# One scan for both values of a step, and an accumulating DMA for the token stream

## The chip, the cores and the metric

The kernel runs on one core of a Trainium2 chip. Times are device microseconds (us). The time before is 2727.75 us, the median of 3 runs (2727.06 to 2733.11).

## What is computed

Two layers work on x of 8 batches x 512 tokens x 256 features, all in float32. Each adds an attention part and a feed-forward part to its input. The change is in the attention part of the first layer, a linear recurrence that runs over the tokens in both directions:

```python
dx = conv(x) - x                                  # neighbours, per feature
t5 = tanh((x + dx * maa_x) @ maa_w1)              # five groups of 32
xw, xk, xv, xr, xg = (x + dx * (maa_f + t5[f] @ maa_w2[f]) for f in range(5))
r, k, v, g = xr @ Wr, xk @ Wk, xv @ Wv, silu(xg @ Wg)
d = exp(-exp(time_decay + tanh(xw @ decay_w1) @ decay_w2))
# forward, per head: S = d_t * S + k_t v_t ; y_f = r_t S
# backward:          y_b = r_t S ; S = d_t * (S + k_t v_t)
y = y_f + y_b
out = (group_norm(y * sigmoid(dx @ gate_w + gate_b)) * g) @ Wo
```

There are 16 heads of 16 x 16 state. Beside it the first layer has 8 experts, of which each token uses 2. The second layer has two softmax attentions and 16 small experts.

## The kernel before

Five queues run in their written order: PE (TensorE), DVE (VectorE), ACT (ScalarE) and SP (SyncE, which issues DMAs) are pinned to the order in which the code records instructions; POOL (GpSimd) is not, and a scheduler places its instructions. Work is written as Python generators. `Turns.turn` moves each running generator to its next `yield`, so a turn decides what stands beside what in each queue, and the number of `yield`s between a producer and a consumer says how much other work is put between them.

The first layer's spine is `scans`. Features lie on partitions, tokens run along the free dimension. A step treats one batch b, one half c of the 256 features and one pair vg of the 16 value columns of a head: 8 x 2 x 8 = 128 steps. In a step, SP's eight DMAs of `spread` (L878) have brought the two values of each head to its 16 partitions as `kv`, 128 x 2 x 512. DVE multiplies by k (L901), then for each of the two values runs a forward scan with the factors `dq` (L910) and a backward scan with the decays `d` (L914), and multiplies by r (L923). The two scans together give the sum of both directions up to factors that k and `dq` hold. PE then adds up over the 16 partitions of each head (`sums`, L929). A step has four `yield`s, so four turns.

Beside the scans run: `experts`, 39 chunks of 256 routed tokens, with weights that POOL gathers from memory by indirect DMA (`wgu`, `wdn` L567, tokens `xs` L577), products on PE (L615, L655), silu on ACT (L639), products on DVE (L624); `projections(b + 1)`, which prepares the next batch one part after the other (`inputs`, `values`, `decays`); and `ending`, which normalises a finished half and multiplies it by g on POOL (L987).

`projections` is what the change touches. `mixed` makes the inputs xw ... xg: PE's product goes to PSUM (L732, L734), DVE computes (product + maa) * dx into a tile `xf` of 128 x 512 (L739), and POOL adds the token stream xT to it (L742). Two turns later PE reads the tiles: `dw` (L815) reads xw, and `project` (L697) makes r, v, k and g of the others. `values` calls `mixed` for xv and xk, `decays` for xw and xr, and later for xg. `decays` makes `d` on ACT (L829, L830), with one column more that holds 0 for the last token, and `dq` on DVE (L848 to L854). Batch 0 is prepared before the scans begin; there the mixing tiles lie in buffers of the pool `held`, and the routing and its `turn_round` (a table of which token is in which slot, made by comparing and multiplying one-hot tiles `ls` and `hs`) go through DVE, ACT and PE too. `entry` starts the second layer: it gathers each token's two expert rows as `y0`.

Of the kernel before, what the change touches and what calls it, by code (L numbers as in the profile page):

```python
# [26 lines left out]
F32 = mybir.dt.float32  # L27
# [9 lines left out]
P = 128  # L37
B, T, D = 8, 512, 256
NC = D // P
# [126 lines left out]
def two_layers(ctx: ExitStack, tc: tile.TileContext, a: dict, out: bass.AP):  # L166
# [106 lines left out]
    def entry(b):  # L273
# [7 lines left out]
        for t0 in range(0, NT, ahead):  # L281
            ys = []
            for t in range(t0, t0 + ahead):
                y = temp([P, 2, D], "y0", f"y0_{b}_{t}", ahead)
                n = b * NT + t
                for i in range(2):
                    pool_e.indirect_dma_start(
                        out=y[:, i, :], out_offset=None, in_=outs,
                        in_offset=bass.IndirectOffsetOnAxis(ap=slot[i][:, n : n + 1], axis=0),
                    )  # L290
                ys.append((t, n, y))
            yield
# [79 lines left out]
    with ExitStack() as l0:  # L372
# [142 lines left out]
        def turn_round():  # L515
# [18 lines left out]
            for k in range(NTT // 4 + 1):  # L534
# [9 lines left out]
                if k < NTT // 4:  # L544
                    ls = held(k % 4, [P, 2, 4, P], f"ls{k}")
                    hs = held(4 + k % 4, [P, 2, 4, n2], f"hs{k}")
                    for i in range(2):
                        for o, of in ((ls, low), (hs, high)):
                            n = o.shape[3]
                            vec_e.tensor_tensor(  # L550
                                o[:, i], bc(of[i][:, 4 * k : 4 * k + 4], 2, n),
                                bc(C["count"][:, :n], 1, 4), ALU.is_equal,
                            )
                    for j in range(4):
                        n = 4 * k + j
# [114 lines left out]
        made = {}  # L670

        def projections(b):

# [13 lines left out]

            def mix(name, i, other=False):
                if other and first:
                    return held(i, [P, T], f"{name}_{b}")  # L690
                return rw.tile([P, T], F32, tag="xf", name=f"{name}_{b}", bufs=4)

# [29 lines left out]
            def mixed(*fs, other=False):  # L722

                xs = {f: [] for f in fs}
                for c in range(NC):
# [10 lines left out]
                    yield  # L736
                    for f, ps in zip(fs, pss):
                        t = mix(f"xf{f}{c}", 2 * c + (f != fs[0]), other)
                        vec_e.scalar_tensor_tensor(  # L739
                            t, ps, V("maa_" + "wkvrg"[f], c), dxs[c], ALU.add, ALU.mult  # L740
                        )
                        pool_e.tensor_tensor(t, t, xT[c], ALU.add)  # L742
                        xs[f].append(t)
                yield
                yield
                return [xs[f] for f in fs]

            def inputs():
# [13 lines left out]
                for _ in range(0 if first else 1):  # L762
                    yield
                xxx = []
                for c in range(NC):
                    t = mix(f"xxx{c}", c)
                    vec_e.scalar_tensor_tensor(t, dxs[c], V("maa_x", c), xT[c], ALU.mult, ALU.add)
                    xxx.append(t)
                for _ in range(1 if first else 2):
# [37 lines left out]
            def decays():  # L807
                yield from until("inputs", b)
                d = rw.tile([P, NC, T + 1], F32, tag="d", name=f"d_{b}", bufs=2)
                vec_e.memset(d[:, :, T:], 0.0)  # L810
# [17 lines left out]
                for co in range(NC):  # L828
                    act_e.activation(dT[:, co, :], pss[co], AF.Exp, bias=V("time_decay", co))  # L829
                act_e.activation(dT, dT, AF.Exp, scale=-1.0)  # L830
                for _ in range(1 if first else 2):
                    yield
# [5 lines left out]

                near = [mix(f"near{c}", 4 + c, True) for c in range(NC)]
                for c in range(NC):  # L840
# [3 lines left out]
                for _ in range(1 if first else 2):  # L844
                    yield
                dq = big("dq")
                for c in range(NC):
# [5 lines left out]
                vec_e.scalar_tensor_tensor(dq, dq, -1.0, q[:, :, 1:], ALU.mult, ALU.mult)  # L853
                vec_e.tensor_tensor(dq, dq, dT, ALU.mult)  # L854
                yield
                yield from until("keys", b)
                k = made[b]["k"]
                vec_e.tensor_tensor(k, k, q[:, :, 1:], ALU.mult)
                made[b].update(d=d, dq=dq, r=r)
                done.add(("scans", b))  # L860
# [8 lines left out]

        NV = 2  # L870
        STEPS = P // (P // HD) // NV

        def spread(b, c, vg):

            kv = rw.tile([P, NV, T], F32, tag="kv", name=f"kv{c}{vg}_{b}", bufs=4)
            for hh in range(P // HD):
                row = c * P + hh * HD + vg * NV
                nc.sync.dma_start(  # L878
                    kv[hh * HD : (hh + 1) * HD], bc(made[b]["vd"][row : row + NV, :], 0, HD)
                )  # L880
            return kv


# [3 lines left out]
        def scans(turns):  # L887
# [4 lines left out]
            for n, (b, c, vg) in enumerate(todo):  # L892
                if c == vg == 0:
                    x = rw.tile([P, NT, D], F32, tag="x", name=f"x_{b}")
                    z = rw.tile([P, NC, T], F32, tag="z", name=f"z_{b}")
                    if b + 1 < B:
                        turns.add(then(*projections(b + 1)))
                k, d, dq, r = (made[b][n] for n in ("k", "d", "dq", "r"))
                dc, qc, kc, rc = d[:, c, 1:], dq[:, c, :], k[:, c, :], r[:, c, :]
                kv = kvs.pop((b, c, vg))  # L900
# [7 lines left out]
                yield  # L908
                for i in range(NV):
                    vec_e.tensor_tensor_scan(  # L910
                        out=kv[:, i, :], data0=qc, data1=kv[:, i, :], initial=0.0,
                        op0=ALU.mult, op1=ALU.add,
                    )
                    vec_e.tensor_tensor_scan(  # L914
                        out=kv[:, i, ::-1], data0=dc[:, ::-1], data1=kv[:, i, ::-1],
                        initial=0.0, op0=ALU.mult, op1=ALU.add,
                    )
                    if i == 0 and len(late) == 2:
                        for sums in late:
                            sums()  # L920
                        late = []
                    yield
                vec_e.tensor_tensor(kv, kv, bc(rc, 1, NV), ALU.mult)  # L923
# [96 lines left out]
        def begin():  # L1020
# [8 lines left out]
            tag_of = {  # L1029
                "y0": ("xf", 4), "gt4": ("t5a", 1), "eq4": ("th", 1), "gt16": ("dx", 1),  # L1030
                "eq16": ("xnT", 1), "cT": ("xf", 4),
            }
# [511 lines left out]
```

## Time and profile before

| what | value |
|---|---|
| median of 3 runs | 2727.75 us |
| the profiled execution | 2728.59 us |
| its span, first to last instruction | 2726.8 us |
| PE, DVE, ACT, POOL busy | 2362.4, 2157.0, 888.3, 477.5 us |
| scans L914 and L910 | 336.7 and 320.0 us on DVE, 256 instructions each |
| multiplications L901 and L923 | 172.0 and 162.9 us on DVE, 128 each |
| additions L742 | 113.3 us on POOL, 80 |
| mean granted PE clock | 0.916 |

A line of the profile names the source line, the engine, the operation and the tiles (written <- read). Where it has a bar, the busy time and the mean duration of one follow, then the idle time of the engine before it and what ended it. A wait line names who waited for whom, the total in us, the number of times and the longest. The rows of digits cut the span into 40 equal slices of 68 us, and each digit is the busy share in tenths.

### The profile page before, as it was taken

Reading aid. Unit: us, or ns where it says so; the run is one execution under the profiler, and the core shown is the slowest. Engines: PE = TensorE matmul, PEld = TensorE weight load, DVE = VectorE, ACT = ScalarE, POOL = GpSimd, SP = SyncE. Lnnn points to the kernel's source line nnn. Section 1 sums busy time; section 2 is a strip of 40 time slices with the busy share of each in tenths; the row PEclk is TensorE's granted clock in tenths of the full one; section 3 lists DMA queues with packets and bytes.
Section 4 is the critical chain, followed back from the end, with each engine's and each line's share of the span. In section 5 each row is a group of like instructions: output and inputs, shape, how many; then the busy total and the mean of one; then the engine's idle time right before and its main releaser. Section 6 shows DMA issues by size and latency. Waiting matters only on the chain.

```text
span 2726.8 us, 32763 instructions
## 1 busy us (share of the span) xinstructions
PE 2362.4 (87%) x11900; PEld 1412.8 (52%) x11900; DVE 2157.0 (79%) x3063; ACT 888.3 (33%) x1687; POOL 477.5 (18%) x441
## 2 busy tenths in 40 slices
PE   6699898988989889898826899999989989898996
PEld 4355555555556545555503445555555555555554
DVE  7799999899999989989985755656576675756666
ACT  1233232222323123231102334434333434434344
POOL 2132232322223223232012100010010101001000
PEclk9688998989889899999957899999989989998998
DMA  6335455455465544655443100000010111000000
GB/s 219 112 104 148 141 176 148 142 146 156 138 176 153 158 133 138 173 151 140 138 122 104 43 16 17 20 27 25 20 36 20 32 32 31 25 24 21 20 9 17
DMA packets 100832, 248.87 MB, mean 91 GB/s; under 512 B 24992, under 2 KB 50368, under 8 KB 95552
## 3 DMA queue, kind: packets, MB, share of 16 engines
q1 hardware_dynamic: 70528, 113.32, 15.0%
q0 software_dynamic: 21168, 115.75, 13.6%
q10 hardware_dynamic: 8976, 17.69, 1.8%
q8 instruction: 96, 1.57, 0.2%
q14 instruction: 64, 0.52, 0.1%
HBM read 215.22 MB, written 31.46 MB: 90 GB/s over the span
## 4 chain that ended last, share of the span: by engine, by line
PE 57%; DVE 25%; DMA 6%; issue 6%; ACT 2%; SPq 2%; POOL 1%; DVEq 0%; ACTq 0%; POOLq 0%
PE y L1427 6%; PE y L655 6%; PE g L1381 5%; DMA kv<-vd 5%; PE g L615 4%; PE u L1381 4%; PE u L615 4%; DVE kv L910 3%; PE sc_g L1279 2%; DVE kv L901 2%; PE ys L929 2%; PE o_g L1307 2%; DVE kv L914 2%; PE qkv_l L1171 2%; SPq L878 2%
## 5 line engine op out<-in xcount | busy, mean ns | idle before, releaser
L914 DVE TENSOR_TENSOR_SCAN kv<-d,kv 128x512 f32<-128x512 f32 x256 | 336.7, 1315 | 8.8
L655 PE MATMUL y<-wdn,h 128*128 128x256 f32 x936 | 286.6, 443 | 54.9 <-DVE h L624 50.5
L910 DVE TENSOR_TENSOR_SCAN kv<-dq,kv 128x512 f32<-128x512 f32 x256 | 320.0, 1250 | 3.4
L655 PEld LDWEIGHTS y<-wdn,h 128*128 128x128 f32 x936 | 180.6, 211 | 186.6 <-issue 83.5
L1287 ACT ACTIVATE pt_g<-sc_g 128x512 f32<-128x512 f32 (+1 forms) x384 | 171.2, 531 | 275.0 <-PE sc_g L1279 215.3
L615 PE MATMUL g<-xsT,wgu 128*128 128x256 f32 x936 | 229.2, 388 | 4.7 <-ACT h L639 3.2
L1381 PE MATMUL g<-xT,w 128*128 128x512 f32 x384 | 203.7, 656 | 25.9 <-DVE att_l L1335 14.0
L615 PEld LDWEIGHTS g<-xsT,wgu 128*128 128x128 f32 x936 | 176.1, 192 | 57.4 <-issue 27.4
L1381 PE MATMUL u<-xT,w 128*128 128x512 f32 x384 | 188.5, 614 | 10.7 <-ACT qkT_g L1239 6.0
L615 PE MATMUL u<-xsT,wgu 128*128 128x256 f32 x780 | 196.3, 392 | 0.0
L1427 PE MATMUL y<-w,h 128*128 128x256 f32 x768 | 183.6, 392 | 0.7 <-ACT qkT_g L1239 0.7
L901 DVE TENSOR_TENSOR kv<-kv,k 128x1024 f32<-128x1024 f32 x128 | 172.0, 1344 | 6.6 <-DMA kv<-vd 6.6
L615 PEld LDWEIGHTS u<-xsT,wgu 128*128 128x128 f32 x780 | 149.5, 195 | 51.4 <-issue 22.8
L923 DVE TENSOR_TENSOR kv<-kv,r 128x1024 f32<-128x1024 f32 x128 | 162.9, 1273 | 3.6
L929 PE MATMUL ys<-kv,cst 128*32 128x512 f32 x512 | 105.7, 701 | 65.4 <-DVE kv L923 65.1
L1399 DVE TENSOR_TENSOR h<-h,u 128x512 f32<-128x512 f32 x96 | 66.0, 688 | 121.5 <-PE u L1381 116.6
L1427 PEld LDWEIGHTS y<-w,h 128*128 128x128 f32 x768 | 144.4, 193 | 34.2 <-issue 11.2
L639 ACT ACTIVATE h<-g 128x512 f32<-128x512 f32 (+1 forms) x117 | 61.7, 527 | 272.6 <-PE g L615 262.5
L1293 DVE TENSOR_TENSOR pt_g<-pt_g,cst 128x512 f32<-128x512 f32 x128 | 85.2, 686 | 75.1 <-ACT pt_g L1287 75.1
L742 POOL TENSOR_TENSOR xf<-xf,xnT 128x512 f32<-128x512 f32 x80 | 113.3, 1436 | 124.1 <-DVE xf L739 123.8
L1381 PEld LDWEIGHTS g<-xT,w 128*128 128x128 f32 x384 | 72.6, 201 | 110.7 <-issue 84.8
L1287 ACT ACTIVATE pt_l<-sc_l 128x384 f32<-128x384 f32 (+1 forms) x256 | 98.0, 469 | 86.3 <-PE sc_l L1279 70.7
(307 smaller groups left out, 3874.5 us busy)
## 6 DMA issues: line engine op xcount, KB each, us to landing
kv<-vd SPq DMA_DIRECT2D x1024, 64.0 KB
cb<-cd SPq DMA_DIRECT2D x128, 128.0 KB
outs<-ys POOLq DMA_DIRECT2D x39, 256.0 KB
w<-in_w ACTq DMA_DIRECT2D x12, 384.0 KB
xn<-in_x SPq DMA_DIRECT2D x8, 512.0 KB
xnT<-xT ACTq DMA_DIRECT2D x16, 256.0 KB
normed<-xn SPq DMA_DIRECT2D x8, 512.0 KB
xnT<-xnT SPq DMA_DIRECT2D x8, 512.0 KB
```

Of the source, the lines that this page charges most:

```text
L615: pe.matmul(o, w[:, at + c * P : at + (c + 1) * P], xT[:, c, :], start=c == 0, stop=c == NC - 1,)
L655: pe.matmul(y[:, n, :], hs[j // 2][lo:, j % 2, n * P : (n + 1) * P], wd[lo:, j * D : (j + 1) * D], start=j == 0, stop=j == NJ0,)
L742: pool_e.tensor_tensor(t, t, xT[c], ALU.add)
L901: vec_e.tensor_tensor(kv, kv, bc(kc, 1, NV), ALU.mult)
L910: vec_e.tensor_tensor_scan(out=kv[:, i, :], data0=qc, data1=kv[:, i, :], initial=0.0, op0=ALU.mult, op1=ALU.add,)
L914: vec_e.tensor_tensor_scan(out=kv[:, i, ::-1], data0=dc[:, ::-1], data1=kv[:, i, ::-1], initial=0.0, op0=ALU.mult, op1=ALU.add,)
L923: vec_e.tensor_tensor(kv, kv, bc(rc, 1, NV), ALU.mult)
L929: pe.matmul(y[r0 : r0 + 32, :], C["take"][:, 24 - 8 * at : 56 - 8 * at], kv[:, i, :], start=at == 0, stop=at == 3, skip_group_check=True,)
L1287: act_e.activation(pt[:, i, :end], scs[i][:, :end], AF.Exp, scale=0.25)
L1293: vec_e.tensor_tensor(pt[:, :, a0 : a0 + m], pt[:, :, a0 : a0 + m], bc(mask[:, :m], 1, 4), ALU.mult,)
L1381: pe.matmul(ps, w[:, k, c * P : (c + 1) * P], xT[:, c, :], start=c == 0, stop=c == NC - 1,)
L1427: pe.matmul(y[:, i, :], hs[k][:, (t + i) * P : (t + i + 1) * P], w1[j - 5 + k][:, 2, :], start=k == 0, stop=k == 5,)
```

## The change

The change has five parts.

- `mixed` writes both halves c of an input into one tile of 128 x 2 x 512, and POOL issues one DMA per input that adds the token stream onto it (`accum_op=ALU.add`). No engine's arithmetic adds it. Two more turns pass before PE reads the tile (one more in batch 0).
- `twice` makes copies of the decays and of `dq` on ACT in which each row stands twice, 128 x 2 x 512 a half: four copies a batch.
- `scans` then runs one forward and one backward scan of 1024 elements over both values of a step, where two of 512 each ran. At the seam the factor is 0: the last column of `d` is 0 before too, and the first of `dq` is now set to 0 on POOL. The four turns of a step stay, with one scan in each of two turns.
- `d` and `dq` have one buffer instead of two, the one-hot tiles `ls` and `hs` two instead of four, and the tiles with tag `xf` are two of double size.
- `entry` gathers y0 two token tiles at a time into a tile of double size.

```diff
@@ -280,15 +280,16 @@
         ahead = 2 if b else NT
         for t0 in range(0, NT, ahead):
             ys = []
-            for t in range(t0, t0 + ahead):
-                y = temp([P, 2, D], "y0", f"y0_{b}_{t}", ahead)
-                n = b * NT + t
-                for i in range(2):
-                    pool_e.indirect_dma_start(
-                        out=y[:, i, :], out_offset=None, in_=outs,
-                        in_offset=bass.IndirectOffsetOnAxis(ap=slot[i][:, n : n + 1], axis=0),
-                    )
-                ys.append((t, n, y))
+            for t in range(t0, t0 + ahead, 2):
+                y = temp([P, 2, 2, D], "y0", f"y0_{b}_{t}", ahead // 2)
+                for j in range(2):
+                    n = b * NT + t + j
+                    for i in range(2):
+                        pool_e.indirect_dma_start(
+                            out=y[:, j, i, :], out_offset=None, in_=outs,
+                            in_offset=bass.IndirectOffsetOnAxis(ap=slot[i][:, n : n + 1], axis=0),
+                        )
+                    ys.append((t + j, n, y[:, j]))
...
@@ -542,8 +543,8 @@
                             )
                     last = None
                 if k < NTT // 4:
-                    ls = held(k % 4, [P, 2, 4, P], f"ls{k}")
-                    hs = held(4 + k % 4, [P, 2, 4, n2], f"hs{k}")
+                    ls = held(k % 2, [P, 2, 4, P], f"ls{k}")
+                    hs = held(2 + k % 2, [P, 2, 4, n2], f"hs{k}")
                     for i in range(2):
                         for o, of in ((ls, low), (hs, high)):
                             n = o.shape[3]
@@ -686,9 +690,23 @@
                 return ps_gu.tile([P, T], F32, tag="gu", name=f"{name}_{b}") if first else bank(name)
 
             def mix(name, i, other=False):
+
                 if other and first:
-                    return held(i, [P, T], f"{name}_{b}")
-                return rw.tile([P, T], F32, tag="xf", name=f"{name}_{b}", bufs=4)
+                    return held(i, [P, NC, T], f"{name}_{b}")
+                return rw.tile([P, NC, T], F32, tag="xf", name=f"{name}_{b}", bufs=2)
+
+            def twice(name):
+
+                out = []
+                for c in range(NC):
+                    n = 2 * (name == "dqs") + c
+                    if b % 2 == 0:
+                        out.append(held(4 + n, [P, NV, T], f"{name}{c}_{b}"))
+                    elif n < 2:
+                        out.append(held(1 + n, [P, NV, T], f"{name}{c}_{b}"))
+                    else:
+                        out.append(rw.tile([P, NV, T], F32, tag=f"dqs{c}", name=f"{name}{c}_{b}"))
+                return out
 
             def project(w, xs, co, name, bank=bank):
 
@@ -734,16 +752,15 @@
                             pe.matmul(ps, m2b[64:, cols], t5b, start=True, stop=True)
                         pss.append(ps)
                     yield
-                    for f, ps in zip(fs, pss):
-                        t = mix(f"xf{f}{c}", 2 * c + (f != fs[0]), other)
+                    for f, x, ps in zip(fs, xs, pss):
                         vec_e.scalar_tensor_tensor(
-                            t, ps, V("maa_" + "wkvrg"[f], c), dxs[c], ALU.add, ALU.mult
+                            x[:, c, :], ps, V("maa_" + "wkvrg"[f], c), dxs[c], ALU.add, ALU.mult
                         )
-                        pool_e.tensor_tensor(t, t, xT[c], ALU.add)
-                        xs[f].append(t)
-                yield
-                yield
-                return [xs[f] for f in fs]
+                for x in xs:
+                    pool_e.dma_start(x, xnT[:, :, PAD : PAD + T], accum_op=ALU.add)
+                for _ in range(3 if first else 4):
+                    yield
+                return [[x[:, c, :] for c in range(NC)] for x in xs]
 
             def inputs():
                 pool_e.memset(xnT[:, :, 0:PAD], 0.0)
@@ -806,7 +824,7 @@
 
             def decays():
                 yield from until("inputs", b)
-                d = rw.tile([P, NC, T + 1], F32, tag="d", name=f"d_{b}", bufs=2)
+                d = rw.tile([P, NC, T + 1], F32, tag="d", name=f"d_{b}")
                 vec_e.memset(d[:, :, T:], 0.0)
                 dT = d[:, :, :T]
                 xw, xr = yield from mixed(0, 3, other=True)
@@ -828,6 +846,9 @@
                 for co in range(NC):
                     act_e.activation(dT[:, co, :], pss[co], AF.Exp, bias=V("time_decay", co))
                 act_e.activation(dT, dT, AF.Exp, scale=-1.0)
+                ds = twice("ds")
+                for c in range(NC):
+                    act_e.copy(ds[c], bc(d[:, c, 1:], 1, NV))
                 for _ in range(1 if first else 2):
                     yield
 
@@ -836,14 +857,15 @@
                 vec_e.scalar_tensor_tensor(q, d, 1.0, q, ALU.add, ALU.mult)
                 yield
 
-                near = [mix(f"near{c}", 4 + c, True) for c in range(NC)]
+                both = mix("near", 2, True)
+                near = [both[:, c, :] for c in range(NC)]
                 for c in range(NC):
                     act_e.activation(near[c], q[:, c, :T], AF.Ln, scale=-1.0)
                 for c in range(NC):
                     act_e.activation(near[c], near[c], AF.Exp, scale=-1.0)
                 for _ in range(1 if first else 2):
                     yield
-                dq = big("dq")
+                dq = big("dq", 1)
                 for c in range(NC):
                     vec_e.tensor_tensor(dq[:, c, :], q[:, c, :T], near[c], ALU.mult)
                     vec_e.scalar_tensor_tensor(
@@ -852,11 +874,15 @@
                 yield
                 vec_e.scalar_tensor_tensor(dq, dq, -1.0, q[:, :, 1:], ALU.mult, ALU.mult)
                 vec_e.tensor_tensor(dq, dq, dT, ALU.mult)
-                yield
+                pool_e.memset(dq[:, :, 0:1], 0.0)
+                yield
+                dqs = twice("dqs")
+                for c in range(NC):
+                    act_e.copy(dqs[c], bc(dq[:, c, :], 1, NV))
                 yield from until("keys", b)
                 k = made[b]["k"]
                 vec_e.tensor_tensor(k, k, q[:, :, 1:], ALU.mult)
-                made[b].update(d=d, dq=dq, r=r)
+                made[b].update(ds=ds, dqs=dqs, r=r)
                 done.add(("scans", b))
                 yield
                 (xg,) = yield from mixed(4)
@@ -895,8 +921,9 @@
                     z = rw.tile([P, NC, T], F32, tag="z", name=f"z_{b}")
                     if b + 1 < B:
                         turns.add(then(*projections(b + 1)))
-                k, d, dq, r = (made[b][n] for n in ("k", "d", "dq", "r"))
-                dc, qc, kc, rc = d[:, c, 1:], dq[:, c, :], k[:, c, :], r[:, c, :]
+                k, ds, dqs, r = (made[b][n] for n in ("k", "ds", "dqs", "r"))
+                dc, qc = (x[c].rearrange("p v t -> p (v t)") for x in (ds, dqs))
+                kc, rc = k[:, c, :], r[:, c, :]
                 kv = kvs.pop((b, c, vg))
                 vec_e.tensor_tensor(kv, kv, bc(kc, 1, NV), ALU.mult)
                 if vg == 0:
@@ -906,20 +933,20 @@
                 if n + 1 == len(todo):
                     done.add(("spread",))
                 yield
-                for i in range(NV):
-                    vec_e.tensor_tensor_scan(
-                        out=kv[:, i, :], data0=qc, data1=kv[:, i, :], initial=0.0,
-                        op0=ALU.mult, op1=ALU.add,
-                    )
-                    vec_e.tensor_tensor_scan(
-                        out=kv[:, i, ::-1], data0=dc[:, ::-1], data1=kv[:, i, ::-1],
-                        initial=0.0, op0=ALU.mult, op1=ALU.add,
-                    )
-                    if i == 0 and len(late) == 2:
-                        for sums in late:
-                            sums()
-                        late = []
-                    yield
+                flat = kv.rearrange("p v t -> p (v t)")
+                vec_e.tensor_tensor_scan(
+                    out=flat, data0=qc, data1=flat, initial=0.0, op0=ALU.mult, op1=ALU.add
+                )
+                if len(late) == 2:
+                    for sums in late:
+                        sums()
+                    late = []
+                yield
+                vec_e.tensor_tensor_scan(
+                    out=flat[:, ::-1], data0=dc[:, ::-1], data1=flat[:, ::-1],
+                    initial=0.0, op0=ALU.mult, op1=ALU.add,
+                )
+                yield
                 vec_e.tensor_tensor(kv, kv, bc(rc, 1, NV), ALU.mult)
 
                 def sums(b=b, c=c, vg=vg, kv=kv, y=y, z=z, x=x):
@@ -1027,8 +1054,8 @@
             act_e.dma_start(cbias, a["correction_bias"].to_broadcast([P, E1]))
 
             tag_of = {
-                "y0": ("xf", 4), "gt4": ("t5a", 1), "eq4": ("th", 1), "gt16": ("dx", 1),
-                "eq16": ("xnT", 1), "cT": ("xf", 4),
+                "y0": ("xf", 2), "gt4": ("t5a", 1), "eq4": ("th", 1), "gt16": ("dx", 1),
+                "eq16": ("xnT", 1), "cT": ("xf", 2),
             }
             place_of["bank"] = lambda name: ps_gu.tile([P, T], F32, tag="gu", name=name)
             place_of["temp"] = lambda shape, tag, name, bufs=1: rw.tile(
```

More of the change, by code (lines that the diff above doesn't have):

```diff
@@ L670, in two_layers @@
         made = {}
+        NV = 2
+        STEPS = P // (P // HD) // NV
         def projections(b):
@@ L722, in mixed @@
             def mixed(*fs, other=False):
-                xs = {f: [] for f in fs}
+                xs = [mix(f"xf{f}", i, other) for i, f in enumerate(fs)]
                 for c in range(NC):
@@ L763, in inputs @@
                     yield
-                xxx = []
+                both = mix("xxx", 0)
+                xxx = [both[:, c, :] for c in range(NC)]
                 for c in range(NC):
-                    t = mix(f"xxx{c}", c)
-                    vec_e.scalar_tensor_tensor(t, dxs[c], V("maa_x", c), xT[c], ALU.mult, ALU.add)
-                    xxx.append(t)
+                    vec_e.scalar_tensor_tensor(
+                        xxx[c], dxs[c], V("maa_x", c), xT[c], ALU.mult, ALU.add
+                    )
                 for _ in range(1 if first else 2):
@@ L868, in projections @@
             return inputs(), values(), decays()
-        NV = 2
-        STEPS = P // (P // HD) // NV
         def spread(b, c, vg):
@@ L908, in scans @@
                 yield
-                for i in range(NV):
-                    vec_e.tensor_tensor_scan(
-                        out=kv[:, i, :], data0=qc, data1=kv[:, i, :], initial=0.0,
-                        op0=ALU.mult, op1=ALU.add,
-                    )
-                    vec_e.tensor_tensor_scan(
-                        out=kv[:, i, ::-1], data0=dc[:, ::-1], data1=kv[:, i, ::-1],
-                        initial=0.0, op0=ALU.mult, op1=ALU.add,
-                    )
-                    if i == 0 and len(late) == 2:
-                        for sums in late:
-                            sums()
-                        late = []
-                    yield
+                flat = kv.rearrange("p v t -> p (v t)")
[10 more added lines that the diff above has]
+                    initial=0.0, op0=ALU.mult, op1=ALU.add,
+                )
+                yield
                 vec_e.tensor_tensor(kv, kv, bc(rc, 1, NV), ALU.mult)
```

## The prediction

> **What bounds the kernel now.** I read the page first, then busy time by stretch, then waits in the long stretch, then single lines.
>
> ```profile
> PE   6699898988989889898826899999989989898996
> DVE  7799999899999989989985755656576675756666
> ```
>
> The change lies in the first layer (slices 1 to 21, to some 1424 us), where PE and DVE are both near full. The second layer is PE's, and there the change only packs gathered rows otherwise. The first layer by stretch (busy us of each engine, then PE clock, DMA share, GB/s):
>
> ```profile
> 98.00:160.00 62.00, 38.41 (x159) 26.52 (x160) 59.87 (x103) 15.25 (x38) 6.94 (x7) 0.63 0.34 102
> 160.00:1368.00 1208.00, 1076.24 (x4123) 668.01 (x4122) 1144.68 (x1125) 329.43 (x505) 345.60 (x288) 0.93 0.51 149
> 1368.00:1424.00 56.00, 12.87 (x30) 2.02 (x32) 48.53 (x43) 0.62 (x1) 11.59 (x9) 0.51 0.47 140
> ```
>
> In the middle stretch DVE (third figure) is busy 1144.7 of 1208 us, PE 1076.2. The largest waits there, of DVE and of PE (us, times, longest):
>
> ```profile
> DVE xf L739 <- PE m L732: 34.0, 13, 6.3
> DVE h L624 <- PE u L615: 7.4, 6, 1.8
> ...
> PE y L655 <- DVE h L624: 50.5, 27, 5.1
> PE ys L929 <- DVE kv L923: 20.4, 11, 3.9
> ```
>
> DVE's waits sum to 43.1 us; 1208 - 1144.7 - 43.1 leaves 20.2 us of short gaps. So DVE is occupied for 1164.9 us, and PE has 88.7 us less to do. DVE bounds, with PE close behind.
>
> **The change part by part: scans.** The scans of a step, undisturbed (start, us):
>
> ```profile
> 508.88 1.22 DVE L910 TENSOR_TENSOR_SCAN kv<-dq,kv 128x512 f32<-128x512 f32 x1
> 510.14 1.22 DVE L914 TENSOR_TENSOR_SCAN kv<-d,kv 128x512 f32<-128x512 f32 x1
> 511.28 1.20 DVE L910 TENSOR_TENSOR_SCAN kv<-dq,kv 128x512 f32<-128x512 f32 x1
> 512.51 1.22 DVE L914 TENSOR_TENSOR_SCAN kv<-d,kv 128x512 f32<-128x512 f32 x1
> 513.77 1.22 DVE L923 TENSOR_TENSOR kv<-kv,r 128x1024 f32<-128x1024 f32 x1
> ...
> L477 DVE TENSOR_TENSOR_SCAN chto<-one,ch x1: 174/174/174, 106.0 to 106.0; 128x8 f32<-128x8 f32 x1
> ```
>
> Four scans take 513.77 - 508.88 = 4.89 us. The last line, a scan of 8 elements (174 ns), and the median of 512 (1219 ns) give (1219 - 174) / 504 = 2.07 ns an element and 157 ns fixed. One of 1024 is then 2.28 us, and with the 0.04 us that a dependent scan waits here (510.14 - 508.88 against 1.22), two take 4.64. A step gains 0.25 us: two fixed parts, less the 0.08 us by which independent scans overlap. 118 of the 128 steps begin in the middle stretch: 29.5 us. [...]
>
> **The additions leave POOL.** Before, 80 additions stand on POOL at L742, and DVE is slow beside them:
>
> ```profile
> 521.70 3.05 POOL L742 TENSOR_TENSOR xf<-xf,xnT 128x512 f32<-128x512 f32 x2 [5.13 <-DVE xf L739]
> 522.19 1.68 DVE L910 TENSOR_TENSOR_SCAN kv<-dq,kv 128x512 f32<-128x512 f32 x1
> 523.90 1.93 DVE L914 TENSOR_TENSOR_SCAN kv<-d,kv 128x512 f32<-128x512 f32 x1
> ...
> L742 POOL TENSOR_TENSOR xf<-xf,xnT x80: 1079/1110/2134, 55.4 to 1239.6; 128x512 f32<-128x512 f32 x80
> ```
>
> The scans here take 1.68 and 1.93 us, not 1.22. Laid against its line's median, every DVE instruction of the trace that is late by more than noise stands beside a POOL addition or product: 44.6 us beside L742, 11.7 beside L987 (which stays), none beside POOL's DMA issues. Of the 44.6 us, 41.8 lie after the start-up. [...] The trace has the loss shared: POOL's additions average 1436 ns against a median of 1110. I take 41.8. [...] The nearest row, POOL's stores at L665, takes 744 to 783 ns in 39 issues among scans, so I add nothing[...].
>
> **What the two are worth.** DVE is occupied for 1164.9 - 29.5 - 41.8 = 1093.6 us, only 17.4 above PE's 1076.2. With PE's spare so small DVE must wait more often. It waited 43 us with 88.7 to spare; I let that grow by half, 20 us (an estimate; its ends are 0, and 71.3 - 17 = 54, at which PE's own waits of 130 us hardly shrink). Gain of the middle: 71.3 - 20 = 51 us.
>
> **What the DMAs cost.** Five a batch, 512 KB each, join the software queue; POOL issues them in two pairs and a single, where ten additions stood, at much the same place among weight loads. Readers: the first PE products of xv (v), xw (dw) and xg (g). Nothing in the trace accumulates. From the software queue's packets, wgu (1.44 MB) lands 7.9 us after issue and wdn (0.79 MB) 5.7, medians: 3.1 us and 3.4 us a MB. As one copy 512 KB takes 4.9 us; if reading the destination counts as a second stream, 6.6. [...] I take 6.6; at a quarter of the wgu rate it would be 10. Before, PE began dw 0.4 to 2.6 us after DVE's last L739, g mostly 0.1 to 4, v mostly 7 to 9. Two turns more are put between; a turn is a quarter of a step, 1208 / 118 / 4 = 2.56 us, so dw has 5.5 to 7.7, g 5.2 to 9, v over 12. So v is hidden, dw late by some 1 us, and g by some 3, as in batches 2, 3, 5 and 6 its issue stands behind a wgu and an xs pair that wait for PE. With 7 batches that is 28 us of PE, behind which its whole queue waits; half of it falls in PE's waits: 14 us. The weight loads behind these DMAs have over 10 us until PE needs them: nothing, unless the transfer is far slower.
>
> **The copies and the zero.** ACT makes four copies of 128x1024 a batch; like its 128x1024 form at L830 (1060 ns) that is 4.2 us, in two lumps of 2.1 before silu work that PE and DVE want. ACT is busy 329 of 1208 us: a quarter of 7 x 4.2 is counted, 7 us (ends 0 and 29). The first column's zero is a POOL memset (0.1 us) between DVE's dq and ACT's copies; in batches 2, 3, 5 and 6 it stands behind that wgu and xs pair, and ACT, in order, may wait there some 5 us with the silu of h behind it and then DVE's product and PE's y, two turns later. That cover leaves little: it is in the 7 us.
>
> **Ends.** Start-up: 2.9 us of disturbance go, four copies before the first scans cost up to 4.2, the one-hot tiles in two buffers instead of four some 1: +2. Tail: six steps at 0.25, -1.5. Freed buffers of d and dq, and y0 in wider tiles, change no bytes and wait for nothing late: 0.
>
> Sum: -51 + 14 + 7 + 2 - 1.5 = -29.5 us on the profiled execution's 2728.6 (span 2726.8): 2699.1. The median of the runs shown is 0.9 lower; I say 2699.
>
> **The rivals.** (1) DVE's time comes through whole: DMAs and copies hide, and 50 to 70 us go: 2658 to 2680. For it: DVE is the bound by 88.7 us; against: only 17.4 remain. (2) Slower: the accumulating transfer is slow, and PE stands before dw and g of each batch. Each us beyond 6.6 costs up to 14 us (7 batches, two readers, both engines now nearly full). Without the 14 us counted, the net is -43.5, so the sign turns at about 6.6 + 3 = 9.7 us; at 12 us it is 14 x 5.4 - 43.5 = +32, 2761; at 10 some 2733. Against: 4.9 to 6.6 by the trace's rates. (3) No change: PE's queue was the bound already where its waits look large, waits simply change sides, and frictions of 20 us eat the rest: 2718 to 2733.
>
> **How the numbers follow.** Forecast 0.58 (2680 to 2718 on its own), rival (1) 0.14, (2) 0.20, (3) 0.08. The kernel's time can be told from no change beyond about 0.2%, 5.5 us. Faster 0.72, same 0.08, slower 0.20. The range, 2662 to 2742, leaves out the far part of (2) and the tip of (1).
>
> **What would show it.** Scans of 128x1024 near 2.28 us, 256 of them; no late DVE instruction except beside L987; DVE's busy time in the first layer down by 70 us or more; the first layer's end 30 us earlier. Accumulating DMAs landing 5 to 7 us after issue, PE's waits on them under 30 us. Wrong: scans of 1024 over 2.4 us, PE waits on xf over 60 us, or DVE late beside DMA traffic.

## The result, and the profile after

The changed kernel takes 2699.9 us (median of 4 runs, 2698.1 to 2700.4), beside 2727.7 for the kernel before on the same chip: ratio 0.9893, 95% interval 0.988 to 0.9905. The forecast was 2699. The profiled execution has a span of 2696.3 us, 30.5 less than before. These lines of the page of after answer to the digit rows shown of before:

```profile
PE   6599988889999898998737999998989989898996
DVE  7799989799998978989986655667566766666666
```

The first layer still ends in slice 21, but at 1390.4 us instead of 1423.7. The next view is busy time by stretch, cut at the start of the multiplication by k of step 4 and of step 122 (in each kernel the same work lies between) and at the end of the last step. Columns as before: length, then PE, PE loads, DVE, ACT, POOL, PE clock, DMA share, GB/s. First before, then after:

```profile
97.90:167.40 69.50, 45.81 (x174) 28.65 (x178) 66.55 (x112) 15.94 (x39) 12.75 (x12) 0.65 0.33 97
167.40:1371.10 1203.70, 1068.84 (x4110) 665.89 (x4102) 1141.13 (x1120) 328.74 (x504) 341.62 (x286) 0.93 0.51 150
1371.10:1423.70 52.60, 12.64 (x28) 1.84 (x28) 45.20 (x41) 0.62 (x1) 9.74 (x8) 0.50 0.47 143
```

```profile
101.50:169.20 67.70, 44.10 (x178) 28.30 (x178) 63.93 (x103) 18.18 (x42) 11.20 (x10) 0.68 0.41 105
169.20:1338.70 1169.50, 1047.99 (x4114) 660.01 (x4106) 1067.38 (x884) 351.17 (x528) 342.92 (x259) 0.93 0.62 170
1338.70:1390.40 51.70, 11.57 (x26) 1.65 (x24) 43.89 (x28) 0.62 (x1) 10.89 (x7) 0.50 0.50 143
```

Nearly all of the gain lies in the 118 steps of the middle: 1203.7 to 1169.5, that is 34.2 us. DVE's busy time falls there by 73.8 us and its short gaps (under 150 ns, added up from the trace) from 20.7 to 13.8. So DVE is occupied for 80.7 us less, and only 34.2 arrive. The difference is DVE's waits, 41.8 before and 1169.5 - 1067.4 - 13.8 = 88.3 after. The largest waits of DVE and PE in after, 160 to 1340 us:

```profile
DVE xf L756 <- PE m L750: 32.2, 15, 7.4
DVE yg L977 <- PE ys L956: 15.4, 7, 4.1
DVE h L625 <- PE u L616: 11.5, 12, 2.2
DVE dq L870 <- ACT near L865: 9.4, 7, 2.0
...
PE y L656 <- DVE h L625: 41.3, 16, 5.7
PE m L752 <- DVE xf L756: 27.4, 7, 7.3
...
PE v L715 <- DMA xf<-xnT: 6.5, 3, 2.7
PE dw L833 <- DMA xf<-xnT: 2.7, 3, 1.2
```

Both engines now wait for each other. No single new wait is large; PE's on the accumulating DMAs are small. PE's 27.4 us at `m` L752 was 2.9 before. PE's own busy time for the same products also fell, from 1068.8 to 1048.0, mostly in `y` and `ys`; the prediction took it as fixed, and why it fell is not shown. The new instructions themselves, from their lines and from the page's list of DMA issues (ns min/median/max for the first three):

```profile
L937 DVE TENSOR_TENSOR_SCAN kv<-dqs,kv x128: 2220/2291/2307, 104.1 to 1384.5; 128x1024 f32<-128x1024 f32 x128
L945 DVE TENSOR_TENSOR_SCAN kv<-ds,kv x128: 2271/2285/2340, 109.9 to 1386.8; 128x1024 f32<-128x1024 f32 x128
L881 ACT COPY dqs<-dq x16: 1038/1043/1047, 100.5 to 1211.5; 128x1024 f32<-128x1024 f32 x16
...
xf<-xnT POOLq DMA_DIRECT2D x40, 512.0 KB, 7.1
```

The scan of 1024 is 2.28 us, the maximum lies within 0.06 us of it (so nothing disturbs a scan any more), and the DMA lands 7.1 us after its issue (the median of the 9 of the 40 whose landing the trace gives).

### The profile page after: what moved, and what is told of

Same layout as the page of the kernel before. It is cut to its first block, busy times and chain, and to the rows that moved or that the text cites. A ratio compares the mean times of both kernels' runs of the same rounds, so it can differ in the third digit from the quotient of the medians.

```text
span 2696.3 us, 32570 instructions
## 1 busy us (share of the span) xinstructions
PE 2341.0 (87%) x11900; PEld 1410.7 (52%) x11900; DVE 2078.6 (77%) x2807; ACT 914.2 (34%) x1715; POOL 473.9 (18%) x409
## 4 chain that ended last, share of the span: by engine, by line
PE 52%; DVE 22%; issue 11%; DMA 8%; ACT 3%; POOL 2%; SPq 1%; ACTq 0%; DVEq 0%; POOLq 0%
PE y L1454 6%; PE g L1408 5%; PE y L656 5%; PE u L1408 4%; PE g L616 4%; DMA kv<-vd 3%; PE u L616 3%; PE sc_g L1306 2%; DMA xf<-xnT 2%; DVE kv L945 2%; DVE kv L937 2%; PE o_g L1334 2%; PE qkv_l L1198 2%; PE ys L956 2%; PE sc_l L1306 1%
## 5 line engine op out<-in xcount | busy, mean ns | idle before, releaser
L656 PE MATMUL y<-wdn,h 128*128 128x256 f32 x936 | 272.6, 428 | 43.7 <-DVE h L625 41.3
L937 DVE TENSOR_TENSOR_SCAN kv<-dqs,kv 128x1024 f32<-128x1024 f32 x128 | 292.1, 2282 | 3.1
L945 DVE TENSOR_TENSOR_SCAN kv<-ds,kv 128x1024 f32<-128x1024 f32 x128 | 292.8, 2287 | 1.6
L1408 PE MATMUL g<-xT,w 128*128 128x512 f32 x384 | 197.2, 638 | 27.0 <-DVE att_l L1362 14.0
L950 DVE TENSOR_TENSOR kv<-kv,r 128x1024 f32<-128x1024 f32 x128 | 165.3, 1291 | 3.4
L928 DVE TENSOR_TENSOR kv<-kv,k 128x1024 f32<-128x1024 f32 x128 | 156.0, 1219 | 12.9 <-DMA w<-in_w 7.2
L1454 PEld LDWEIGHTS y<-w,h 128*128 128x128 f32 x768 | 144.5, 194 | 34.7 <-issue 11.2
L956 PE MATMUL ys<-kv,cst 128*32 128x512 f32 x512 | 96.8, 669 | 50.1 <-DVE kv L950 50.1
L578 POOL DMA_INDIRECT xs<-normed,whose x78 | 122.2, 1566 | 77.6 <-DVE whose L562 47.5
```

Of the source, the lines that this page charges most:

```text
L578: pool_e.indirect_dma_start(out=xs[:, n, :], out_offset=None, in_=normed, in_offset=bass.IndirectOffsetOnAxis(ap=whose[:, at : at + 1], ax ...
L656: pe.matmul(y[:, n, :], hs[j // 2][lo:, j % 2, n * P : (n + 1) * P], wd[lo:, j * D : (j + 1) * D], start=j == 0, stop=j == NJ0,)
L928: vec_e.tensor_tensor(kv, kv, bc(kc, 1, NV), ALU.mult)
L937: vec_e.tensor_tensor_scan(out=flat, data0=qc, data1=flat, initial=0.0, op0=ALU.mult, op1=ALU.add)
L945: vec_e.tensor_tensor_scan(out=flat[:, ::-1], data0=dc[:, ::-1], data1=flat[:, ::-1], initial=0.0, op0=ALU.mult, op1=ALU.add,)
L956: pe.matmul(y[r0 : r0 + 32, :], C["take"][:, 24 - 8 * at : 56 - 8 * at], kv[:, i, :], start=at == 0, stop=at == 3, skip_group_check=True,)
```

## The experiments

All twelve kernels were timed against the kernel before. "Occupied" and "waits" are DVE's in the 118 middle steps of the profiled execution, worked out as above; the last column is the ratio of times with its 95% interval. Occupied and waits belong to one execution each: those of `scans_only` and `xg_later` are the longest of their runs, 8 and 11 us above the median, and that of `before_turns` is the shortest, 6 us below it. A difference of a few us between waits says little.

| kernel | scans | turns after mixing | stream added by | occupied | waits | ratio |
|---|---|---|---|---|---|---|
| before | 512 | 2 | POOL | 1161.9 | 41.8 | 1 |
| before_turns | 512 | 4 | POOL | 1161.2 | 40.8 | 1.0 (0.9992-1.0009) |
| dma_only | 512 | 4 | DMA | 1122.7 | 71.1 | 0.9965 (0.9952-0.9978) |
| scans_only | 1024 | 2 | POOL | 1122.2 | 90.3 | 0.9994 (0.9986-1.0003) |
| scans_turns | 1024 | 4 | POOL | 1114.6 | 72.9 | 0.9938 (0.9922-0.9953) |
| after_two_turns | 1024 | 2 | DMA | 1081.9 | 182.1 | 1.0229 (1.0214-1.0244) |
| after | 1024 | 4 | DMA | 1081.2 | 88.3 | 0.9893 (0.988-0.9905) |
| no_add | 1024 | 4 | nothing | 1080.7 | 77.1 | 0.9839 (0.9826-0.9851) |
| one_copy | 1024 | 4 | DMA | 1081.6 | 86.7 | 0.9876 (0.9861-0.989) |
| dve_zero | 1024 | 4 | DMA | 1081.3 | 90.0 | 0.9891 (0.9872-0.9909) |
| scans_dve_zero | 1024 | 2 | POOL | 1117.6 | 79.9 | 0.9987 (0.9974-1.0) |
| scans_xg_later | 1024 | 2 (+2) | POOL | 1123.2 | 84.4 | 1.0001 (0.999-1.0012) |
| xg_later | 1024 | 4 (+3) | DMA | 1079.6 | 136.2 | 1.0014 (1.0004-1.0024) |
| xg_bank | 1024 | 4 | DMA | 1080.7 | 88.9 | 0.988 (0.9864-0.9897) |

### The two halves of the change alone

`scans_only` has merged scans, copies and the zero, and leaves the additions on POOL. Its edit to the changed kernel:

```diff
-                for x in xs:
-                    pool_e.dma_start(x, xnT[:, :, PAD : PAD + T], accum_op=ALU.add)
-                for _ in range(3 if first else 4):
-                    yield
+                        pool_e.tensor_tensor(x[:, c, :], x[:, c, :], xT[c], ALU.add)
+                yield
+                yield
```

> The doubled decay rows and the merged scans stay; the additions go back to POOL (80 of 128x512), with the two turns that stood there before. Theory (DVE's time is what is saved, and DVE has only 88 us over PE to give): DVE loses 32 us of scans and the POOL additions disturb it as before, so some 15 to 25 us of the 32 come through: 2703 to 2713. Rival (most of the change's gain is the additions leaving POOL): within 8 us of the kernel before, 2720 to 2730. Second rival: with scans twice as long a POOL addition and a scan shut each other out for longer, so the additions, not the scans, lengthen to 2 to 3 us each and PE waits on them.

Measured: 2728.7 us, no gain: a miss. The additions average 1.63 us there (1.44 before), below the 2 to 3 us of the second rival. `dma_only` is the kernel before with the accumulating DMA and its two more turns; the four scans of 512 stay:

```diff
-                        pool_e.tensor_tensor(t, t, xT[c], ALU.add)
+                for x in xs:
+                    pool_e.dma_start(x, xnT[:, :, PAD : PAD + T], accum_op=ALU.add)
+                for _ in range(3 if first else 4):
+                    yield
```

> The accumulating DMA and its two further turns alone, with scans of 512 on single rows, no copies on ACT and no zero on POOL. Theory: 42 us of disturbance on DVE go, DMA lateness and more waiting take half: 2705 to 2715. If the two parts are independent, their gains add up to the change's 28 us; if both draw on the same spare of PE, the sum of the single gains is well above 28 (each alone near 20).

Measured: 2716.8 us, 2 us slower than the expected range. The halves give 0 and 11 us, the whole 28. Both outcomes that were thought of failed: the gains do not add up, and the halves are not near 20 each but less than the whole. DVE's occupied time does add up (39.7 by the scans, 39.2 by the DMA kernel, 80.7 together), so the missing 17 us are waits: in `scans_only` they ate all of it.

### What the additions and the copies still cost

`no_add` leaves the accumulating DMAs out:

```diff
-                for x in xs:
-                    pool_e.dma_start(x, xnT[:, :, PAD : PAD + T], accum_op=ALU.add)
```

> The changed kernel without the addition of the token stream (left out altogether, the turns stay): what the accumulating DMAs cost. My forecast put 14 us on their lateness: 2683 to 2690 if that holds. Rival (they are hidden, since PE waits only 10 us on them in the trace): 2695 to 2700.

Measured: 2684.1 us, as expected. The DMAs cost 0.54% of 2727, about 15 us, where the prediction had 14. `one_copy` makes the doubled rows in batch 0 only and leaves out those of the other batches, which then use batch 0's:

```diff
-                ds = twice("ds")
-                for c in range(NC):
-                    act_e.copy(ds[c], bc(d[:, c, 1:], 1, NV))
+                if first:
+                    rows["ds"] = twice("ds")
...
-                pool_e.memset(dq[:, :, 0:1], 0.0)
+                if first:
+                    pool_e.memset(dq[:, :, 0:1], 0.0)
```

> The changed kernel with the doubled rows of batch 0 used for all batches (copies of batches 1 to 7 and their zero on POOL left out): what ACT's copies and ACT's 32 us of waiting behind POOL's zero cost. My forecast: 7 us, 2690 to 2695. Rival (ACT has room enough): 2697 to 2700. Other rival (ACT waiting in order is what made DVE's waits double): 2675 to 2688.

Measured: 2693.7 us, 5 to 6 less than after; the two intervals overlap, so the copies and the zero are small but not sized exactly. `dve_zero` moves the zero alone, since ACT waits 36.3 us for it:

```diff
-                pool_e.memset(dq[:, :, 0:1], 0.0)
+                vec_e.memset(dq[:, :, 0:1], 0.0)
```

> The changed kernel with the zero of the first column written by DVE instead of POOL. ACT's waits for POOL there are 36.3 us in 8 pieces. If they delay the silu behind them: 2692 to 2697. If they are hidden: 2698 to 2701. DVE pays some 0.1 us for each of 8.

Measured: 2696.1 us. That lies in the range of the first theory, but its ratio, taken against the kernel before on its own chip, is 0.9891 against 0.9893: no difference. ACT's wait for POOL's zero costs nothing that shows in the changed kernel.

### Why the merged scans need the two turns

Three kernels asked what took the scans' gain in `scans_only`. `scans_dve_zero` has the zero on DVE there (the edit of `dve_zero`):

> The merged scans alone, POOL additions kept, but the first column's zero written by DVE instead of POOL. Merged scans alone gave 2728.7 us, nothing. Theory Z: ACT's copies stood behind POOL's zero, which stood behind POOL's additions and its gathers that wait for PE (PE waited 26.9 us for ACT's silu there); with the zero on DVE these 20 to 27 us come back: 2702 to 2714. Theory T: the gain is missing for want of the two turns in which the additions can finish: 2725 to 2731, no change. Theory X: long scans and POOL additions shut each other out longer: 2722 to 2731 also.

`scans_turns` is the changed kernel with POOL's additions in place of the DMAs, its turns kept:

```diff
-                for x in xs:
-                    pool_e.dma_start(x, xnT[:, :, PAD : PAD + T], accum_op=ALU.add)
+                        pool_e.tensor_tensor(x[:, c, :], x[:, c, :], xT[c], ALU.add)
```

> The changed kernel with POOL's additions in place of the accumulating DMAs; the two more turns stay. Theory Z (the zero blocks ACT because POOL is late with additions): little comes back, 2718 to 2730. Theory T (two turns were missing, the mixed inputs come late from POOL): PE's waits for them go, 2700 to 2712. Theory X (additions and long scans shut each other out, some 46 us of DVE): 2720 to 2728, DVE late by 40 us or more beside the additions.

`before_turns` is the kernel before with the turns alone:

```diff
-                yield
-                yield
+                for _ in range(3 if first else 4):
+                    yield
```

> The kernel before with nothing but the two more turns after the mixing (one more in batch 0). Theory T: the turns by themselves are worth something, 2712 to 2722, as much as the DMA kernel without merged scans (2716.8). Otherwise they are neutral or shift the groups of work against each other: 2724 to 2733.

Measured: 2723.6, 2710.2 and 2728.2 us. The zero is hardly it (at most 7 us). The turns alone are worth nothing. With merged scans they are worth 0.56%, 15 us: the time of theory T, though not by its reason, since in `scans_only` PE waits just 7.2 us for POOL's additions. Of the 46 us of DVE in theory X, 33 are there (1114.6 occupied in `scans_turns`, 1081.2 in after), but the time lies below its range. At four turns the change is additive within the intervals: scans 0.62% with POOL's additions, and 0.72% with DMAs; the DMA 0.35% with old scans and 0.45% with new.

What happens at two turns stands in the timeline of `scans_only`, batch 1, step 6 (start, us; in brackets the idle time before and who ended it):

```profile
344.68 0.37 ACTq L814 DMA_DIRECT2D vd<-v  x1
...
351.48 1.13 PE L750 MATMUL m<-t5a,m2a 32*128 32x512 f32 x4
...
356.70 1.23 DVE L927 TENSOR_TENSOR kv<-kv,k 128x1024 f32<-128x1024 f32 x1 [7.23 <-DMA kv<-vd]
357.96 1.41 DVE L756 SCALAR_TENSOR_TENSOR xf<-m,vecs,dx 128x512 f32<-128x512 f32 x2
...
358.76 2.07 PE L750 MATMUL m<-t5a,m2a 32*128 32x512 f32 x3 [4.67 <-DVE xf L756]
```

DVE waits 7.2 us for the next kv, its L756 stands behind that, and PE's next `m` waits for L756 to free the PSUM bank. The next `ys` stand in PE's order behind that `m`; in `scans_turns` they come ahead of it. Why kv is late stands in what DVE and SP wait for, 160 to 1340 us of `scans_only`:

```profile
DVE kv L927 <- DMA kv<-vd: 17.5, 4, 7.2
...
SPq L901 <- DMA vd<-v: 50.9, 7, 14.6
```

SP issues seven of the eight kv transfers of this step by 341.8 us. The last goes out at 349.4, when the store of the next batch's v (`vd`, L814) has landed. SP's trace has this wait once in each of the first seven batches, 5.0 to 14.6 us long. It falls into the transfers of step 6, and DVE then waits for kv in batches 1, 2, 4 and 5 (7.2, 2.2, 6.2 and 1.9 us). In `scans_turns`, where v comes two turns later, it falls into those of step 7, and DVE's waits for kv are gone: about 17 us, as much as the two kernels' waits differ by. The kernel before has it at step 7 in batches 1 and 4 and for 3.8 us at step 6 in 2 and 5, and DVE does not wait for kv there. Why a kv transfer has to wait for that store is not shown.

Another wait of `scans_only` was tested by itself: PE stood 26.9 us at the second xg product, for a PSUM bank that ACT's sd (`ending`) frees. `scans_xg_later` moves the mixing of xg past it:

```diff
+                for _ in range(0 if first else 2):
+                    yield
                 (xg,) = yield from mixed(4)
```

> The merged scans alone (POOL additions, two turns, the zero on POOL; 2728.7 us) with two turns put ahead of the mixing of xg alone, so that both its products go to PE after sd has freed its bank and ahead of rs. Theory A (the shared PSUM bank between the mixing of xg and `ending`): PE's wait on ACT's sd (26.9 us) goes to under 5, and the time to 2708 to 2716. Theory B (POOL's additions were late for v, k, w and r too): 2722 to 2730.

Measured: 2726.5 us. The wait for sd is gone, the time is not: theory A falls for this kernel. PE now stands 25.1 us at `ys` for DVE's kv (6.5 in `scans_only`), and DVE's 6.7 us for kv in batches 1 and 4 are still there. By elimination the turns matter at the earlier mixings. The waits for `vd` point to that of xv and xk; moving it alone was not tried.

### The same turns and the DMA

`after_two_turns` has two turns in the changed kernel:

```diff
-                for _ in range(3 if first else 4):
-                    yield
+                yield
+                yield
```

> The changed kernel with two turns after the mixing, as before, instead of four (batch 0: two instead of three). Theory A (with two turns ACT's copies of dq stand ahead of the sd of `ending`, and PE's second xg product waits for the bank that sd frees; this, not the additions, took the gain of the merged scans away): that wait is back with 20 to 27 us, and the DMAs, 7.1 us after issue, are now awaited too: PE waits on xf from DMAs of 40 us or more; 2712 to 2728. Theory B (the two turns only matter to POOL's additions, which are gone): 2698 to 2706, at most the 5 us of lateness a DMA more.

Measured: 2789.1 us, 89 slower than after, 62 slower than before: far beyond either theory. PE's waits in it, 160 to 1340 us:

```profile
PE m L752 <- ACT sd L998: 30.5, 5, 9.6
PE g L715 <- DMA xf<-xnT: 26.3, 7, 8.4
PE y L656 <- DVE h L625: 22.2, 13, 3.5
PE dw L833 <- DMA xf<-xnT: 22.2, 5, 5.9
PE v L715 <- DMA xf<-xnT: 16.7, 3, 5.7
```

PE stands 65 us before g, dw and v for the DMAs, and DVE waits 94 us longer than in after. With PE and DVE both near full, such a wait comes through. It is the mechanism of rival (2), reached by taking 5.1 us of cover away instead of by a slower transfer. At the 14 us per us of that rival, an estimate, it would be 72 us. The rest is not settled. DVE's wait for kv is back, 29.2 us where after has 5.7; PE's 30.5 us for sd are not in after either, but taking such a wait out of `scans_only` gained nothing. Two turns with the DMA and the old scans were not tried.

### PE's 27 us at the second xg product

In after, `rs` of `ending` stands in PE's order between the two products of xg, and all use a PSUM ring of two buffers, so the second product waits until DVE has read the first. `xg_later` moves xg past `rs`:

```diff
+                for _ in range(0 if first else 3):
+                    yield
                 (xg,) = yield from mixed(4)
```

> The changed kernel with three turns put ahead of the mixing of xg, so that rs no longer takes the second bank between its two products, where PE waits 27.4 us in 7 pieces for DVE to read the first. Theory A: that wait goes to under 5 us; DVE and PE are both near full, so about half of it comes through: 2684 to 2692. Theory B (the wait is hidden, PE has to wait for DVE anyway): 2697 to 2702.

Measured: 2731.7 us, 32 slower than after and outside both theories. The wait at `m` is gone, but PE now waits 41.9 us before g. POOL's timeline of `xg_later` beside the scans of batch 1, where DVE ended the xf of xg at 412.3:

```profile
418.73 1.35 POOL L568 DMA_INDIRECT wdn<-in_w_dn,wrow  x1 [9.96 <-PE y L656]
420.08 0.78 POOL L666 DMA_DIRECT2D outs<-ys  x1
420.85 1.32 POOL L760 DMA_DIRECT2D xf<-xnT  x1
430.26 0.10 POOL L766 MEMSET xnT<- 128x4 f32 x1 [8.09 <-DMA xf<-xnT]
```

The DMA is issued 8.6 us after its data are ready, because in POOL's order it now follows a weight gather that waits for PE's y. Beside batches 1, 2, 4 and 5 the issue is 5.8 to 8.6 us late. After it, POOL itself waits: the memset of the next batch's xnT may not overwrite what the DMA reads. Three more turns made the DMA later.

`xg_bank` leaves the turns alone and takes another PSUM ring for these products:

```diff
-                        ps = (other_bank if other else bank)(f"m{f}{c}")
+                        if f == 4:
+                            ps = ps_gu.tile([P, T], F32, tag="gu", name=f"m{f}{c}_{b}")
+                        else:
+                            ps = (other_bank if other else bank)(f"m{f}{c}")
```

> The changed kernel with the two products of xg in the four-buffer PSUM ring of the experts instead of the two-buffer bank that `ending` shares; the turns, and so POOL's issue of the accumulating DMA, stay where they are. In the changed kernel PE waits there 27.4 us in 7 pieces. Theory A: that wait is worth half its length (PE and DVE are both near full), PE's wait for m falls under 5 us, and the time is 2684 to 2693. Theory B: the wait only moves, to the next product of the ring or to the experts' y behind DVE's h: 2696 to 2704. Theory C: the ring is turned by two and the experts' products collide in it: over 2706.

Measured: 2695.2 us, between the ranges of theories A and B; the ratio of 0.988 cannot be told from after. PE's waits in it:

```profile
PE y L656 <- DVE h L625: 40.4, 16, 5.7
PE ys L959 <- DVE kv L953: 21.9, 16, 4.5
PE xsT L588 <- DVE h L625: 14.4, 4, 5.7
```

Against after, `ys` has grown by 10.5 us and `xsT` from 0.8 to 14.4: 24 of the 27.4 us moved to the next products that need DVE. That is what theory B says: there PE merely runs ahead of DVE, and a wait of PE is free. None of these kernels beats after by more than the measurement can tell, except the one that does not add.

## Why the prediction was right

What the prediction counted on is there: DVE loses 80.7 us of work, PE is next, waits eat a good half of it, and the DMAs cost some 15 us. That the forecast met the median within a us is luck, for its terms were not that close:

| term (us) | predicted | measured |
|---|---|---|
| start-up, to step 4 | +2 | +1.8 (167.4 to 169.2) |
| scans, DVE occupied | -29.5 | -41.5 (dma_only to after) |
| additions' disturbance, DVE occupied | -41.8 | -38.5 (before_turns to dma_only) |
| DVE's waits from little room | +20 | +35.3 (before to no_add) |
| DMAs | +14 | +11.2 in waits, about 15 in time (no_add to after) |
| copies and zero | +7 | +1.6 in waits (already in the 35.3), 5 to 6 in time (one_copy to after) |
| tail | -1.5 | -0.9 (52.6 to 51.7) |
| second layer | 0 | +2.8 |

`no_add` makes the copies too, so the 1.6 is not counted twice: the occupied times and the waits add up to -33.5, the middle itself gained 34.2, and the prediction had -30. Two errors nearly cancel, the scans and the room:

- **Scans.** "Two take 4.64 us" was too much. The duration was right (2.28), but each counted until DVE's next instruction, waits left out, the two occupy 4.52 us a step in after. The prediction put the two directly behind each other; only 21 of the 118 steps have them so. Elsewhere other work stands between them: the second starts without the 0.04 us of a dependent one, and in 63 of the other 97 steps that work overlaps the first by some 0.08.
- **Room.** "I let that grow by half, 20 us" was too little. `no_add` has neither additions nor DMAs, and its DVE waits 35.3 us more than before. In the whole change, taking 81 us off the engine that binds brought back 46 in waits; PE, with its 1048 us of 1169, was next.
- **Disturbance.** It went as forecast: of the 41.8 us read from the trace, 38.5 came back, and of 9 us left of it in after, all but noise lie beside the product L1014. Both engines paid, as the prediction's lines at 521.70 show: two scans that begin under an addition last 0.46 and 0.71 us longer, and the two additions 0.83 us longer in sum. In the trace of before, all 47 scans that begin under a POOL addition or product, over 0.1 us after its start, end 1.08 to 1.09 us after it (undisturbed, a scan takes 1.22); of the 22 additions that begin so under a scan, 21 end 0.88 to 0.89 us after it (the shortest addition takes 1.08).
- **The DMA.** 6.6 us was the author's estimate, from the landings of wgu and wdn (7.9 and 5.7 us) and an assumed second stream; 7.1 was measured, and what an accumulating DMA does inside is not shown: a plain store of 256 KB from the same queue (`outs`) also takes 6.6 us. The 9 known landings lie between 5.1 and 10.2 us. An issue takes 1.34 us beside scans of 1024 and 1.33 beside those of 512 (`dma_only`), medians, where the stores that the prediction went by took 0.74 to 0.78. The total was right, its readers were not: v, said to be hidden, waits most (6.5 us), dw 2.7, and g 3.9 us once, in batch 0. The two turns are the cover: without them it is +89 us, with what the merged scans lose there included.
- **The zero.** ACT waits 36.3 us in 8 pieces, some 5 each as said, and nothing follows from it.

Of the rivals, (1), that DVE's time comes through whole, failed: 80.7 us went and 34.2 arrived. (2) named a mechanism that exists, and `after_two_turns` shows how near it lay. (3), that waits eat the gain, is what `scans_only` did. What the prediction did not see is that the scans' gain does not stand by itself: the same two turns that cover the DMA also keep the merged scans' kv from being late.

## What to carry to other kernels

When two engines are both near full (here 97% and 89% of the middle), add up what the bound engine is occupied with, and then expect a good part of a saving back as waits: here 46 of 81 us. The occupied time of the two edits added, their waits did not. A turn count is a part of an edit like any instruction: test it apart, because it covers latency at one place and moves bank and queue order at others. Before removing a wait, look which engine runs ahead there: a wait of the one with room moves to the next product, and a DMA moved later may be issued behind something that blocks its queue.

## What the runs showed of the hardware

- POOL's product beside the longer scans. Its median went from 1966 to 3098 ns; at its shortest it takes 1261. A scan now lasts 2.28 us, and 11 of the 16 products begin under one and end 1.05 to 1.07 us after it. In the timeline of after:

```profile
402.78 2.27 DVE L945 TENSOR_TENSOR_SCAN kv<-ds,kv 128x1024 f32<-128x1024 f32 x1
403.01 3.10 POOL L1014 TENSOR_TENSOR z<-z,g 128x512 f32<-128x512 f32 x1
...
405.08 2.11 DVE L950 TENSOR_TENSOR kv<-kv,r 128x1024 f32<-128x1024 f32 x1
```

  The product starts 0.2 us after the scan, whose 2.27 us are undisturbed, and ends 1.1 us after the scan's end; the multiplication that follows pays, 2.11 us for 1.22. The loss that is left is 8.6 us on L950.
- POOL's gathers also take longer to issue beside the long scans: `xs` 1566 ns on average, 1207 before, and 1536 in `scans_only`, which has the long scans without the DMAs. An accumulating DMA takes 1342 ns to issue and a plain store 772 (medians). POOL had the room.
